# Cross-attention with sparsemax and a cosine/sine layer: the three products of the 32-token tile on four column tiles, with new order constants

## The chip, the core and the metric

The kernel runs on one core of a Trainium2 chip. The core has five engines that run side by side and meet through semaphores: PE (TensorE, matrix products; its weight loads are a row of their own in the profile, PEld), DVE (VectorE), ACT (ScalarE), POOL (GpSimd) and SP (SyncE, which here only issues transfers). The metric is the device time of one execution in microseconds. Before the change, three runs gave 622.4, 619.33 and 619.13, median 619.33.

## What is computed

Eight batches of 100 query tokens with 512 features attend to 722 context tokens each, in 16 heads of 32 features. The weights come from sparsemax (a threshold tau is subtracted from each row of scores, and what is negative becomes zero) in place of softmax. Then a layer with the cosine of one matrix and the sine of another follows. Cut to what matters:

```python
def sparsemax(x):                      # x: (8, 16, 100, 722)
    ...                                # tau so that the clipped row sums to 1
    return jnp.clip(x - tau, 0.0)

qh, kh, vh = heads(layernorm(x) @ Wq + bq), heads(ctx @ Wk + bk), heads(ctx @ Wv + bv)
attn = sparsemax(einsum('bhqd,bhkd->bhqk', qh, kh) * 32 ** -0.5)
x = x + merge(einsum('bhqk,bhkd->bhqd', attn, vh)) @ Wo + bo
real = layernorm(x) @ cos(theta + theta_noise)
imag = layernorm(x) @ sin(phi + phi_noise)
out = x + sqrt(real * real + imag * imag)
```

All of it is in 32-bit floats.

## The kernel before

**Tiles of tokens.** The 800 query tokens (8 x 100) are cut into seven tiles, `TILES = (128, 128, 128, 32, 128, 128, 128)` (line 29), across the batches' borders. What is done per token (norm, queries, output product, residual, second norm, cosine and sine products, root, result) is done per tile. The fourth tile, tokens 384 to 415, has only 32 tokens; its last steps can start when batch 4 (tokens 400 to 499) has its attention outputs.

**A batch.** What is done per batch: keys (`keys`, four products into eight pieces) and values (`values`, six pieces of the context); five `fill`s of scores into the four-bank PSUM tile `psc`, each copied to SBUF by ACT (`fill copy`, tile `s_t`) and searched by DVE (`tops`, the eight largest of each of 24 segments, 16 MAX8 instructions at a time). From the candidates DVE makes a first bound, and five rounds improve it: `above` (DVE compares candidates with the bound), `above values` (POOL multiplies), `above count` (DVE counts), `update` or `update far` (DVE sums POOL's product and moves the bound). `parts` (POOL), `parts T` (PE) and `parts copy` (ACT) bring the bounds into place for `weights` (PE: scores again, minus the bound, five groups into `psc`), `weights relu` (ACT) and `outputs` (PE). The last batch makes its bounds in three portions, so that its weights can begin earlier.

**The tile's last steps.** `last_steps` (line 934) adds for each tile: `output product` (line 936, `product` with `wo_sb`), `load x again` and `add bo`, `residual` (DVE adds the product in PSUM to x), the second norm with its transposition and copy, two `ffn` products with `cos_sb` and `sin_sb`, a `square` of each on ACT, their sum on POOL, the square root on ACT, and `result`, in which POOL adds x and sends the rows out. `product` (line 499) has the tile's transposed activations as weights of the array (128 x tokens) and streams 512 columns of the matrix, in four chunks of 128 features that add up in PSUM. A matmul in 32-bit floats is two records in the profile, so one product is 8 records. With the 32-token tile only 32 of the array's 128 columns hold weights.

[...]

**What sets the order.** Nothing is issued where it is written. `add` makes a `Task` with its engine and an assumed cost from `STEPS` (line 93); `hold` states which buffer slots it takes and which tasks free them. `Plan.order` (line 275) then plays the program through with these assumed costs. On each engine the task that can start first is taken; among those that can start at the same moment, the one with the smallest `due`:

```python
t.due = t.batch * PERIOD - t.rank + LAG.get(t.kind, 0.0)
stay = STAY if engine == "PE" and t.shape == shape else 0.0
key = (max(start, now + WINDOW), t.due - stay)
```

`rank` is the assumed length of what depends on the task, `LAG` (line 157) a constant per kind of task, `STAY` (line 154) a bonus for a PE task of the shape that the array has just had, `PERIOD` (line 155) the distance between batches. The tasks are issued in the order of their planned starts; each engine then works through its queue in that order and waits where something isn't ready.

Of the kernel before, what the change touches and what calls it, by code (L numbers as in the profile page):

```python
# [11 lines left out]
FP = mybir.dt.float32  # L12
# [3 lines left out]
AF = mybir.ActivationFunctionType  # L16
ALU = mybir.AluOpType
# [3 lines left out]
B, Q, S, DM = 8, 100, 722, 512  # L21
HD = 32
P = 128
NG = DM // P
HG = P // HD
# [10 lines left out]
FS = 16  # L36
# [7 lines left out]
def fills_of(left_first):  # L44
# [91 lines left out]
    "outputs bias": ("ACT", 0.05, 0.28),  # L136
    "output product": ("PE", 3.43),
    "residual": ("DVE", 0.65),
    "stats 2": ("DVE", 0.85),
    "ffn": ("PE", 3.43),  # L140
    "square": ("ACT", 0.57),
# [7 lines left out]
}  # L149


SHAPE = {"fill": 1, "fill last": 2, "outputs": 2, "weights": 3}
CHANGE = (0.19, 0.1, 0.1, 0.1)
STAY = 175.0
PERIOD = 121.0
WINDOW = 0.0
LAG = {
    "above": 260.0,
    "above count": -180.0,
    "above values": -150.0,  # L160
    "add bo": -5.0,
    "bounded": -75.0,
    "candidates": -190.0,
    "checks": 30.0,
    "deviation": 165.0,
    "ffn": 300.0,
    "fill": -240.0,
    "fill copy": 30.0,
    "fill last": -235.0,
    "first bound": 270.0,  # L170
    "keys": -65.0,
    "keys bias": 280.0,
    "keys part": -285.0,
    "leftovers": 250.0,
    "load bias": 205.0,
    "load ctx": 295.0,
    "load part": 120.0,
    "load w": 200.0,
    "load x": -160.0,
    "load x again": 180.0,  # L180
    "losses": 250.0,
    "normed": -80.0,
    "normed 2": -110.0,
    "normed T": -65.0,
    "normed copy": -245.0,
    "output product": 235.0,
    "outputs": -205.0,
    "outputs bias": 70.0,
    "parts": -180.0,
    "parts T": -165.0,  # L190
    "parts copy": -240.0,
    "parts copy last": -285.0,
    "queries": -285.0,
    "queries bias": -215.0,
    "residual": -55.0,
    "rests": 130.0,
    "result": 150.0,
    "sines": -300.0,
    "square": -215.0,
    "square sum": 275.0,  # L200
    "stats": 100.0,
    "stats 2": 265.0,
    "tops": 240.0,
    "turned": 160.0,
    "turns": -255.0,
    "update": 55.0,
    "update far": 155.0,
    "values": 110.0,
    "values copy": -200.0,
    "weights": -80.0,  # L210
    "weights relu": 300.0,
}


# [13 lines left out]
class Plan:  # L228
# [9 lines left out]
    def add(self, kind, emit, *after, tiles=1):  # L238
        t = Task(kind, emit, after, tiles)
        t.batch = self.batch  # L240
        self.tasks.append(t)
        for a in after:
            self.edge(a, t)
        return t
# [78 lines left out]
def xattn_ffn(  # L323
# [18 lines left out]
    nc = tc.nc  # L342
# [47 lines left out]
    def load_ctx_part(st, b, c):  # L390
# [4 lines left out]
    wq_sb, wk_sb, wv_sb, wo_sb, cos_sb, sin_sb = (  # L395
        const.tile([P, NG, DM], FP, name=n)
        for n in ("wq_sb", "wk_sb", "wv_sb", "wo_sb", "cos_sb", "sin_sb")
    )
# [88 lines left out]
    def queries_bias(tk, pieces):  # L487

        for st, at, q, n in pieces:
            if "q" not in st:  # L490
                st["q"] = work.tile([P, NG, Q], FP, name="q_t", bufs=3)
            nc.vector.tensor_tensor(
                st["q"][:, :, q : q + n],
                tk["pq"][:, :, at : at + n],
                bq_sb[:, :, None].to_broadcast([P, NG, n]),
                ALU.add,
            )

    def product(tk, name, lhs, w_sb):
        tk[name] = ps1.tile([P, DM], FP, name="pm")[: tk["n"]]  # L500
        for c in range(NG):
            nc.tensor.matmul(  # L502
                tk[name],
                lhsT=tk[lhs][:, c, :],
                rhs=w_sb[:, c, :],
                start=(c == 0),
                stop=(c == NG - 1),
            )

    def residual(tk):  # L510
        nc.vector.tensor_tensor(tk["x"], tk["py"], tk["x"], ALU.add)

    def square(tk, k):
        tk["sq", k] = rows.tile([P, DM], FP, name="sq", tag="sq", bufs=2)[: tk["n"]]
        nc.scalar.activation(tk["sq", k], tk["pr", k], AF.Square)  # L515

    def square_sum(tk):
        nc.gpsimd.tensor_tensor(tk["sq", 0], tk["sq", 0], tk["sq", 1], ALU.add)  # L518

    def root(tk):  # L520
        nc.scalar.activation(tk["sq", 0], tk["sq", 0], AF.Sqrt)
# [354 lines left out]
    add, hold = plan.add, plan.hold  # L876
# [56 lines left out]

    def last_steps(tk, outs):

        py = add("output product", lambda: product(tk, "py", "oT", wo_sb), *outs, *w["o"])
        xi = add("load x again", lambda: set_x(tk), tk["normed"])
        bo_in = add("add bo", lambda: add_bo(tk), xi, w["bo"])
        rs = add("residual", lambda: residual(tk), py, bo_in)
        hold("pm", py, [rs])  # L940
        _, hT2_in, hT2 = norm_steps(tk, rs, " 2")
        prs, sqs = [], []
        for k, w_sb in enumerate((cos_sb, sin_sb)):
            pr = add(
                "ffn",
                lambda k=k, w_sb=w_sb: product(tk, ("pr", k), "hT", w_sb),
                hT2, sines_done[k],
            )
            s = add("square", lambda k=k: square(tk, k), pr)
            hold("pm", pr, [s])  # L950
            prs.append(pr)
            sqs.append(s)
        hold("hT", hT2_in, prs)
        ss = add("square sum", lambda: square_sum(tk), *sqs)
        rt = add("root", lambda: root(tk), ss)
        at, n = tk["at"], tk["n"]
        rz = add("result", lambda: result(tk, out.rearrange("b q d -> (b q) d")[at : at + n]), rt)
        hold("n_t", sqs[0], [rz])
        hold("n_t", sqs[1], [ss])
        hold("x", xi, [rz])  # L960
        return py

    w = {}
    sines_done, turned_before = [], []
    for b in range(B):
# [30 lines left out]
        for g in range(NG):  # L996
            for i in range(2):
                early = b == 0 and 2 * g + i < EARLY
                if early:
                    k = first_keys[-1]  # L1000
                else:
                    k = add("keys", lambda st=st, g=g, i=i: keys(st, g, i), *c_in, *w["k"])
# [10 lines left out]
        for n, (pieces, _) in enumerate(st["fills"]):  # L1013
            cs = [c for c, *_ in pieces]
            if LEFT in cs:
                f = add("fill last", lambda st=st, n=n: fill(st, n), ql_in, *q_in, *ks.values())
                hold(f"ql{par}", ql_in, [f])
            else:
                gs = {divmod(HG * c + k, QB)[0] for c in cs for k in range(HG)}
                f = add(  # L1020
                    "fill", lambda st=st, n=n: fill(st, n), *q_in, *[ks[g, i] for g in gs for i in range(2)],
                    tiles=FS,
                )
            segments = FS if len(cs) == 1 or LEFT not in cs else NC3 * SEG % FS + LS
            e = add("fill copy", lambda st=st, n=n: fill_copy(st, n), f, tiles=segments)
            fills.append(f)
            hold("psc", f, [e])
            ts = [
                add("tops", lambda st=st, n=n, j=j: tops(st, n, j), e, tiles=segments)
                for j in range(HG)  # L1030
            ]
            hold("s", e, ts)
            for c in cs:
                done_tops[c] += ts
            top_steps += ts
# [4 lines left out]
        for lo, hi in ((0, HG + 1), (HG + 1, 2 * HG + 1), (2 * HG + 1, NT)) if b == B - 1 else ((0, NT),):  # L1040
# [8 lines left out]
            for reach in REACH:  # L1049
                m = add("above", lambda st=st, r=r: above(st, **r), t, tiles=hi - lo)  # L1050
                p = add("above values", lambda st=st, r=r: above_values(st, **r), m, tiles=hi - lo)
                n = add("above count", lambda st=st, r=r: above_count(st, **r), m, tiles=hi - lo)
# [3 lines left out]
                    p, n, tiles=hi - lo,  # L1056
# [39 lines left out]
        outs, ws, all_o, first_o = [], [], [], {}  # L1096
        for n, pairs in enumerate(PAIRS):
# [4 lines left out]
                tiles=len(pairs),  # L1102
# [57 lines left out]
        for tk, at, q, n in st["out"]:  # L1160
# [6 lines left out]
            if tk["at"] + tk["n"] <= (b + 1) * Q:  # L1167
                py = last_steps(tk, tk["outs"])
# [33 lines left out]
    again = small.tile([1, 1], I32, name="again", bufs=1)  # L1202
    nc.vector.tensor_scalar(again, most, 0.5, None, ALU.is_gt)
    flag = nc.values_load(again[0:1, 0:1], min_val=0, max_val=1)
    with tc.If(flag > 0):
        with tc.For_i(0, B) as b:
            st = {"c": load_ctx(b)}
            tk = {"x": load_x(x[ds(b, 1)].rearrange("o q d -> q (o d)"), Q), "n": Q}
# [25 lines left out]
            for c in range(NC3 + 1):  # L1234
# [4 lines left out]
                for j in range(HG if c < NC3 else 1):  # L1239
                    n = 1 + HG * c + j if c < NC3 else 0  # L1240
# [88 lines left out]
```

## Time and profile before

The execution that was profiled took 617.21 us, of which the span from first to last instruction is 615.6.

| | before |
|---|---|
| median of three runs | 619.33 us (619.13 to 622.4) |
| profiled execution | 617.21 us, span 615.6 us |
| mean granted clock of PE | 0.994 of full speed |
| instructions in the span | 17162 |
| HBM traffic | 23.76 MB read, 1.64 MB written |
| chain that ended last | PE 46%, DVE 39%, issue 7%, POOL 5% |

A row of the profile names the engine, the line of the kernel, the operation, the tile written and the tile read, their shapes, and how many such instructions were merged. [...] "Issue" in the chain is time in which the profile shows nothing that was waited for.

### The profile page before, as it was taken

What the parts mean: (1) busy time and instruction counts of PE and PEld (TensorE: products, weight loads), DVE (VectorE), ACT (ScalarE), POOL (GpSimd) and SP (SyncE); (2) the same over time, 40 slices, a digit from 0 to 9 for tenths busy, and PEclk for the clock granted to TensorE, in tenths of its full rate; (3) what the DMA queues carried; (4) which work ended last, traced back from release to release, by engine and by line L of the source; (5) the groups of instructions that cost most, each with busy time, mean ns of one, the idle gap of its engine ahead of it and who ended that gap; (6) DMA issues with size and microseconds to landing.
All of it is one profiled execution on the core that took longest, in us unless ns stands there. A gap on an engine that the chain in (4) does not pass through costs nothing.

```text
span 615.6 us, 17162 instructions
## 1 busy us (share of the span) xinstructions
PE 590.9 (96%) x6497; PEld 330.5 (54%) x6497; DVE 520.5 (85%) x3198; ACT 257.5 (42%) x355; POOL 226.3 (37%) x296
## 2 busy tenths in 40 slices
PE   5999999899999999999999999999999999999974
PEld 3755445556555655566466644675457434555531
DVE  2079999999999999997899989998999899998210
ACT  1244542355354435441644343552545334443521
POOL 1688487765500450024311650025211440165021
PEclk9999999999999999999999999999999999999998
DMA  8920012002000110002010102000030000000000
GB/s 307 364 92 19 18 56 78 18 19 98 19 2 3 40 60 2 3 2 97 19 37 2 41 2 98 3 2 1 3 132 3 0 23 2 2 20 2 2 18 21
DMA packets 12264, 26.56 MB, mean 43 GB/s; under 512 B 1856, under 2 KB 1856, under 8 KB 12176
## 3 DMA queue, kind: packets, MB, share of 16 engines
q1 hardware_dynamic: 11664, 23.77, 11.3%
q0 software_dynamic: 512, 1.64, 0.7%
q8 instruction: 53, 0.87, 0.6%
q14 instruction: 35, 0.29, 0.2%
HBM read 23.76 MB, written 1.64 MB: 41 GB/s over the span
## 4 chain that ended last, share of the span: by engine, by line
PE 46%; DVE 39%; issue 7%; POOL 5%; ACT 1%; DMA 1%; SPq 0%; POOLq 0%; DVEq 0%; ACTq 0%
DVE cand L639 19%; PE pm L581 12%; PE pm L559 12%; PE pm L502 5%; DVE f L727 4%; DVE m L706 4%; PE psc L826 3%; PE pm L849 3%; PE psc L617 3%; DVE n L717 3%; PE pm L479 3%; POOL p L711 3%; PE psc L548 2%; DVE rest L648 1%; DVE t L674 1%
## 5 line engine op out<-in xcount | busy, mean ns | idle before, releaser
L639 DVE MAX8 cand<-s_t 128x8 f32<-128x30 f32 x2496 | 230.3, 174 | 3.5 <-ACT s_t L628 3.5
L711 POOL TENSOR_TENSOR p<-z,m 128x1040 f32<-128x1040 f32 (+2 forms) x50 | 89.1, 1785 | 271.4 <-DVE m L706 269.7
L581 PE MATMUL pm<-wv_sb,c_t 128*121 128x512 f32 (+1 forms) x384 | 174.7, 600 | 0.0
L559 PE MATMUL pm<-c_t,wk_sb 128*128 128x361 f32 x464 | 150.9, 473 | 0.0
L559 PEld LDWEIGHTS pm<-c_t,wk_sb 128*128 128x128 f32 x464 | 84.5, 189 | 52.3 <-issue 7.6
L581 PEld LDWEIGHTS pm<-wv_sb,c_t 128*121 128x121 f32 (+1 forms) x384 | 67.2, 183 | 82.8 <-issue 78.3
L838 ACT ACTIVATE aT<-psc 121x2000 f32<-121x2000 f32 (+1 forms) x40 | 70.8, 1771 | 53.6 <-PE psc L826 53.6
L628 ACT COPY s_t<-psc 128x1924 f32<-128x1924 f32 (+2 forms) x40 | 69.0, 1725 | 47.9 <-DVE cand L639 23.7
L594 ACT COPY v_t<-pm 121x512 f32<-121x512 f32 (+1 forms) x48 | 28.1, 586 | 93.8 <-PE pm L581 93.8
L570 ACT ACTIVATE k_t<-pm,bk_sb 128x361 f32<-128x361 f32 x60 | 33.6, 565 | 71.1 <-PE pm L559 70.9
L727 DVE TENSOR_REDUCE f<-p 128x13 f32<-128x1040 f32 (+2 forms) x50 | 50.7, 1013 | 9.5 <-POOL p L711 9.5
L717 DVE TENSOR_REDUCE n<-m 128x13 f32<-128x1040 bf16 (+2 forms) x50 | 50.7, 1013 | 1.1
L826 PE MATMUL psc<-q_t,k_t 32*121 32x100 f32 (+1 forms) x1536 | 46.8, 262 | 0.0
L849 PEld LDWEIGHTS pm<-aT,v_t 121*32 121x32 f32 (+1 forms) x1536 | 32.7, 109 | 24.7 <-issue 21.7
L826 PEld LDWEIGHTS psc<-q_t,k_t 32*121 32x121 f32 (+1 forms) x1536 | 45.9, 180 | 0.2
L617 PE MATMUL psc<-k_t,q_t 32*32 32x481 f32 (+1 forms) x1536 | 43.2, 474 | 0.0
L849 PE MATMUL pm<-aT,v_t 121*32 121x100 f32 (+1 forms) x1536 | 41.7, 251 | 1.2 <-ACT aT L838 1.2
L479 PEld LDWEIGHTS pm<-hT,wq_sb 128*128 128x128 f32 x224 | 28.2, 191 | 8.2 <-issue 6.3
L479 PE MATMUL pm<-hT,wq_sb 128*128 128x128 f32 (+1 forms) x224 | 29.5, 277 | 0.0
L502 PE MATMUL pm<-cos_sb,hT 128*128 128x512 f32 (+1 forms) x56 | 27.5, 636 | 0.7 <-ACT hT L469 0.7
L518 POOL TENSOR_TENSOR sq<-sq 128x512 f32<-128x512 f32 (+1 forms) x7 | 8.8, 1264 | 48.7 <-ACT sq L515 48.6
L617 PEld LDWEIGHTS psc<-k_t,q_t 32*32 32x32 f32 x1536 | 13.9, 103 | 23.1 <-issue 15.4
(298 smaller groups left out, 570.9 us busy)
## 6 DMA issues: line engine op xcount, KB each, us to landing
c_t<-in_ctx SPq DMA_DIRECT2D x7, 1444.0 KB, 6.3
x_t<-in_x SPq DMA_DIRECT2D x12, 256.0 KB, 2.9
out<-sq POOLq DMA_DIRECT2D x6, 256.0 KB, 2.9
c_t<-in_ctx SPq DMA_DIRECT2D x4, 361.0 KB, 6.2
wk_sb<-in_L_xattn_Wk SPq DMA_DIRECT2D x4, 256.0 KB, 5.5
wq_sb<-in_L_xattn_Wq SPq DMA_DIRECT2D x4, 256.0 KB, 6.3
cos_sb<-in_L_ffn_theta SPq DMA_DIRECT2D x4, 256.0 KB, 3.9
n_t<-in_L_ffn_theta_noise SPq DMA_DIRECT2D x4, 256.0 KB, 3.6
```

Of the source, the lines that this page charges most:

```text
L479: nc.tensor.matmul(tk["pq"][:, g, : tk["n"]], lhsT=wq_sb[:, c, g * P : (g + 1) * P], rhs=tk["hT"][:, c, :], start=(c == 0), stop=(c == NG ...
L559: nc.tensor.matmul(pk, lhsT=wk_sb[:, c, g * P : (g + 1) * P], rhs=st["c"][:, c, i * SH : (i + 1) * SH], start=(c == 0), stop=(c == NG - 1),)
L581: nc.tensor.matmul(pv[:n], lhsT=st["c"][:, k, c * CK : c * CK + n], rhs=wv_sb[:, k, :], start=(k == 0), stop=(k == NG - 1),)
L617: nc.tensor.matmul(psc[b * HD : (b + 1) * HD, j, at : at + EDGE[hi] - EDGE[lo]], lhsT=st["q"][r, g, qb * HD : (qb + 1) * HD], rhs=st["k"][ ...
L628: nc.scalar.copy(s_t[:, :, :n], st["psc"][:, :, :n])
L639: nc.vector.max(st["cand"][:, n, k, :], st["s", f][:, j, at + EDGE[k] - first : at + EDGE[k + 1] - first],)
L711: nc.gpsimd.tensor_tensor(st["p"][:, lo:hi], st["z"][:, lo:hi], st["m"][:, lo:hi], ALU.mult)
L717: nc.vector.tensor_reduce(n_t, st["m"][:, lo:hi], AX.X, ALU.add)
L727: nc.vector.tensor_reduce(s_t, st["p"][:, lo:hi], AX.X, ALU.add)
L826: nc.tensor.matmul(psc[:m, j, k * Q : (k + 1) * Q], lhsT=st["k"][r, g, lo : lo + m], rhs=st["q"][r, g, :], start=False, stop=(k == len(PAI ...
L838: nc.scalar.activation(st["aT", n][:CK, :, :w], st["psw"][:CK, :, :w], AF.Relu, scale=SCALE)
L849: nc.tensor.matmul(st["po", g][j * HD : (j + 1) * HD, :Q], lhsT=st["v"][:m, c, f : f + HD], rhs=aT[:m, j, k * Q : (k + 1) * Q], start=(c = ...
```

## The change

For the tile with 32 tokens (`tk["n"] == HD`) the three products become `small_product`: for each of the four chunks of features, four matmuls take the same 32 columns of weights, each with another 128 of the 512 columns of the matrix, and write to partitions 0, 32, 64 and 96 of the product's PSUM tile. A product is thus 16 matmuls of 128 columns in place of 4 of 512, and its result is 128 x 128 in place of 32 x 512. The residual picks the four pieces out of PSUM one after the other and adds each to its 128 columns of x. Squares and their sum work on the 128 x 128 layout; the root reads the four pieces in turn and puts them back into rows of 512, in the second of the two `sq` buffers, which is therefore held until the result has been sent, while the first is free after the root. Kinds and assumed costs are added for these steps. The assumed cost of a fill that takes scores of two groups is raised by the factor 1.4. `STAY` goes from 175 to 235, `PERIOD` from 121 to 108, and every `LAG` gets a new value, so the order of the whole program is another.

```diff
+    "small product": ("PE", 0.95),
+    "small residual": ("DVE", 0.9),
+    "small square": ("ACT", 0.3),
+    "small sum": ("POOL", 0.45),
+    "small root": ("ACT", 1.1),
...
-SHAPE = {"fill": 1, "fill last": 2, "outputs": 2, "weights": 3}
+SHAPE = {"fill": 1, "fill last": 2, "outputs": 2, "small product": 2, "weights": 3}
-STAY = 175.0
-PERIOD = 121.0
+STAY = 235.0
+PERIOD = 108.0
 LAG = {
-    "above": 260.0,
-    "above count": -180.0,
-    "above values": -150.0,
+    "above": -65.0,
+    "above count": -55.0,
+    "above values": -5.0,
...
-    "ffn": 300.0,
-    "fill": -240.0,
+    "ffn": 245.0,
+    "fill": -300.0,
...
-    "fill last": -235.0,
-    "first bound": 270.0,
-    "keys": -65.0,
+    "fill last": -295.0,
+    "first bound": -180.0,
+    "keys": -60.0,
...
+    "small product": -220.0,
+    "small residual": -245.0,
+    "small root": 300.0,
+    "small square": 175.0,
+    "small sum": -270.0,
...
-    "tops": 240.0,
+    "tops": 300.0,
...
-    "update": 55.0,
-    "update far": 155.0,
-    "values": 110.0,
+    "update": 150.0,
+    "update far": 300.0,
+    "values": 200.0,
...
-    "weights": -80.0,
-    "weights relu": 300.0,
+    "weights": -130.0,
+    "weights relu": -260.0,
...
+    def small_product(tk, name, lhs, w_sb):
+        tk[name] = ps1.tile([P, DM], FP, name="pm")[:, :P]
+        for c in range(NG):
+            for j in range(HG):
+                nc.tensor.matmul(
+                    tk[name][j * HD : (j + 1) * HD],
+                    lhsT=tk[lhs][:, c, :],
+                    rhs=w_sb[:, c, j * P : (j + 1) * P],
+                    start=(c == 0),
+                    stop=(c == NG - 1),
+                )
+
+    def small_residual(tk):
+        for j in range(HG):
+            x_j = tk["x"][:, j * P : (j + 1) * P]
+            nc.vector.tensor_tensor(x_j, tk["py"][j * HD : (j + 1) * HD], x_j, ALU.add)
+
+    def small_square(tk, k):
+        tk["sq", k] = rows.tile([P, DM], FP, name="sq", tag="sq", bufs=2)
+        nc.scalar.activation(tk["sq", k][:, :P], tk["pr", k], AF.Square)
+
+    def small_sum(tk):
+        a, b = tk["sq", 0][:, :P], tk["sq", 1][:, :P]
+        nc.gpsimd.tensor_tensor(a, a, b, ALU.add)
+
+    def small_root(tk):
+
+        for j in range(HG):
+            nc.scalar.activation(
+                tk["sq", 1][:HD, j * P : (j + 1) * P], tk["sq", 0][j * HD : (j + 1) * HD, :P], AF.Sqrt
+            )
+        tk["sq", 0] = tk["sq", 1][:HD]
...
     def last_steps(tk, outs):
-        py = add("output product", lambda: product(tk, "py", "oT", wo_sb), *outs, *w["o"])
+        small = tk["n"] == HD
+        if small:
+            py = add("small product", lambda: small_product(tk, "py", "oT", wo_sb), *outs, *w["o"])
+        else:
+            py = add("output product", lambda: product(tk, "py", "oT", wo_sb), *outs, *w["o"])
...
-        hold("n_t", sqs[0], [rz])
-        hold("n_t", sqs[1], [ss])
+        hold("n_t", sqs[0], [rt] if small else [rz])
+        hold("n_t", sqs[1], [rz] if small else [ss])
...
-                    tiles=FS,
+                    tiles=FS * (1.0 if len(cs) == 1 else 1.4),
```

More of the change, by code (lines that the diff above doesn't have):

```diff
@@ L149 @@
 }
-SHAPE = {"fill": 1, "fill last": 2, "outputs": 2, "weights": 3}
+SHAPE = {"fill": 1, "fill last": 2, "outputs": 2, "small product": 2, "weights": 3}
 CHANGE = (0.19, 0.1, 0.1, 0.1)
-STAY = 175.0
-PERIOD = 121.0
+STAY = 235.0
+PERIOD = 108.0
 WINDOW = 0.0
 LAG = {
-    "above": 260.0,
-    "above count": -180.0,
-    "above values": -150.0,
[L161 to L165, printed above, removed]
-    "ffn": 300.0,
-    "fill": -240.0,
-    "fill copy": 30.0,
-    "fill last": -235.0,
-    "first bound": 270.0,
-    "keys": -65.0,
[L172 to L186, printed above, removed]
+    "above": -65.0,
+    "above count": -55.0,
+    "above values": -5.0,
+    "add bo": -205.0,
+    "bounded": -145.0,
+    "candidates": 40.0,
+    "checks": 150.0,
+    "deviation": -55.0,
+    "ffn": 245.0,
+    "fill": -300.0,
+    "fill copy": -25.0,
+    "fill last": -295.0,
+    "first bound": -180.0,
+    "keys": -60.0,
+    "keys bias": 230.0,
+    "keys part": -130.0,
+    "leftovers": 225.0,
+    "load bias": -100.0,
+    "load ctx": 270.0,
+    "load part": -105.0,
+    "load w": -105.0,
+    "load x": -215.0,
+    "load x again": 55.0,
+    "losses": 270.0,
+    "normed": 95.0,
+    "normed 2": 45.0,
+    "normed T": 65.0,
+    "normed copy": 70.0,
+    "output product": 155.0,
@@ L187 @@
     "outputs": -205.0,
[L188 to L191, printed above, removed]
+    "outputs bias": 200.0,
+    "parts": -215.0,
+    "parts T": -250.0,
+    "parts copy": 290.0,
     "parts copy last": -285.0,
[L193 to L202, printed above, removed]
-    "tops": 240.0,
@@ L204 @@
-    "turned": 160.0,
-    "turns": -255.0,
-    "update": 55.0,
-    "update far": 155.0,
-    "values": 110.0,
-    "values copy": -200.0,
-    "weights": -80.0,
-    "weights relu": 300.0,
+    "queries": -175.0,
+    "queries bias": 115.0,
+    "residual": 270.0,
+    "rests": -40.0,
+    "result": 145.0,
+    "root": -20.0,
+    "sines": -285.0,
+    "small product": -220.0,
[3 more added lines that the diff above has]
+    "small sum": -270.0,
+    "square": -225.0,
@@ L212 @@
+    "square sum": 210.0,
+    "stats": 245.0,
+    "stats 2": -300.0,
+    "tops": 300.0,
+    "turned": 245.0,
+    "turns": 165.0,
+    "update": 150.0,
+    "update far": 300.0,
+    "values": 200.0,
+    "values copy": -40.0,
+    "weights": -130.0,
+    "weights relu": -260.0,
 }
@@ L934, in last_steps @@
     def last_steps(tk, outs):
-        py = add("output product", lambda: product(tk, "py", "oT", wo_sb), *outs, *w["o"])
+        small = tk["n"] == HD
[3 more added lines that the diff above has]
+            py = add("output product", lambda: product(tk, "py", "oT", wo_sb), *outs, *w["o"])
         xi = add("load x again", lambda: set_x(tk), tk["normed"])
         bo_in = add("add bo", lambda: add_bo(tk), xi, w["bo"])
-        rs = add("residual", lambda: residual(tk), py, bo_in)
+        if small:
+            rs = add("small residual", lambda: small_residual(tk), py, bo_in)
+        else:
+            rs = add("residual", lambda: residual(tk), py, bo_in)
         hold("pm", py, [rs])
@@ L944, in last_steps @@
             pr = add(
-                "ffn",
-                lambda k=k, w_sb=w_sb: product(tk, ("pr", k), "hT", w_sb),
+                "small product" if small else "ffn",
+                lambda k=k, w_sb=w_sb: (small_product if small else product)(tk, ("pr", k), "hT", w_sb),
                 hT2, sines_done[k],
             )
-            s = add("square", lambda k=k: square(tk, k), pr)
+            if small:
+                s = add("small square", lambda k=k: small_square(tk, k), pr)
+            else:
+                s = add("square", lambda k=k: square(tk, k), pr)
             hold("pm", pr, [s])
@@ L953, in last_steps @@
         hold("hT", hT2_in, prs)
-        ss = add("square sum", lambda: square_sum(tk), *sqs)
-        rt = add("root", lambda: root(tk), ss)
+        if small:
+            ss = add("small sum", lambda: small_sum(tk), *sqs)
+            rt = add("small root", lambda: small_root(tk), ss)
+        else:
+            ss = add("square sum", lambda: square_sum(tk), *sqs)
+            rt = add("root", lambda: root(tk), ss)
         at, n = tk["at"], tk["n"]
         rz = add("result", lambda: result(tk, out.rearrange("b q d -> (b q) d")[at : at + n]), rt)
-        hold("n_t", sqs[0], [rz])
-        hold("n_t", sqs[1], [ss])
+        hold("n_t", sqs[0], [rt] if small else [rz])
+        hold("n_t", sqs[1], [rz] if small else [ss])
         hold("x", xi, [rz])
```

## The prediction

> **What bounds the kernel now.** I read the page's busy line first, then the busy time by stage (edges at landmarks of the chain of waits), then who waits for whom.
>
> ```profile
> PE 590.9 (96%) x6497; PEld 330.5 (54%) x6497; DVE 520.5 (85%) x3198; ACT 257.5 (42%) x355; POOL 226.3 (37%) x296
> ```
>
> ```profile
> 42.00:366.00 324.00, 320.94 (x3558) 181.47 (x3556) 308.36 (x1868) 142.52 (x190) 139.77 (x162) 1.00 0.09 31
> 366.00:410.00 44.00, 42.74 (x592) 24.79 (x592) 43.37 (x353) 21.75 (x29) 3.42 (x7) 1.00 0.11 36
> 410.00:508.00 98.00, 98.00 (x1040) 52.01 (x1032) 91.88 (x533) 41.79 (x59) 34.44 (x43) 1.00 0.08 26
> 508.00:569.00 61.00, 61.00 (x732) 31.94 (x735) 57.58 (x333) 25.73 (x40) 19.98 (x35) 1.00 0.02 6
> 569.00:590.40 21.40, 20.00 (x342) 12.19 (x334) 3.23 (x11) 10.35 (x13) 1.50 (x9) 1.00 0.01 2
> 590.40:615.60 25.20, 13.24 (x33) 5.54 (x29) 2.70 (x7) 3.68 (x7) 6.19 (x6) 0.86 0.07 24
> ```
>
> Columns: stage, length, then busy us of PE, weight loads, DVE, ACT, POOL, and PE's granted clock. From 42 to 569 us **two engines are full together**: PE has 522.7 of 527 us, DVE 501.2. Of DVE's other 25.8 us, the gaps over 0.4 us in its timeline make 14.3; the rest are steps of some hundredths between instructions. After 569 DVE's search for the bounds is over and PE works off what it still owes.
>
> ```profile
> DVE f L727 <- POOL p L711: 9.5, 15, 1.3
> DVE cand L639 <- ACT s_t L628: 3.5, 4, 1.5
> DVE h_t L455 <- PE pm L463: 3.5, 2, 2.4
> ```
>
> These are DVE's waits that matter inside the full stretch. Summing its timeline's gaps there: some 8.4 us wait for POOL (gaps over 0.4 us before `update`'s reduction, 0.8 each as a rule) and about 5.4 us are PE's lateness (1.05 before a normalisation, 1.83 before a residual, 1.54 and 1.01 before tops). So a faster PE has little DVE idling to remove: its gain must come there and from the tail.
>
> **The products: removed and put in their place.** The tile of 32 tokens has its products at 452.21 (output), 487.48 and 492.90 (ffn).
>
> ```profile
> 487.48 3.62 PE L502 MATMUL pm<-cos_sb,hT 128*32 128x512 f32 x8
> 491.03 0.69 PE L617 MATMUL psc<-k_t,q_t 32*32 32x241 f32 x32
> 491.65 1.46 PE L606 MATMUL psc<-k_t,ql 128*32 128x181 f32 x32
> 492.90 3.60 PE L502 MATMUL pm<-sin_sb,hT 128*32 128x512 f32 x8
> ```
>
> The columns are start, length, engine, line and shape; a start-to-start distance is the price, since lengths overlap. Cosine costs 491.03 − 487.48 = 3.55, sine (to 496.43) 3.53, output 452.21 to 455.67 = 3.46: **10.54 us of PE**. A product is 8 records (4 chunks, 2 each). The new one has 16 matmuls, 32 records of 128 columns into four 32-partition strips. The L606 row above is the same form, 32 records of K=128 and 32 weight columns into four strips, only with 181 columns: 492.90 − 491.65 = 1.25, in other places 1.39 (103.19 to 104.58). Times 128/181 that is 0.88 to 0.98. The outputs give a second row:
>
> ```profile
> 460.66 0.85 PEld L849 LDWEIGHTS pm<-aT,v_t 117*32 117x32 f32 x40 [0.51 <-ACT sd L449]
> 460.66 1.07 PE L849 MATMUL pm<-aT,v_t 117*32 117x100 f32 x40
> ```
>
> Forty records of 100 columns take 1.00 (next line's start, 461.66); times 32/40 and 128/100: 1.02. I take 1.0. Entering strips from full columns costs something: eight value records before strips take 3.63 (541.23 to 544.86), sixteen before others 6.97 (551.44 to 558.41), 3.48 per eight: 0.15. [...] New sum: 3 × 1.0 to 3 × 1.15 = 3.0 to 3.45; **PE saves 7.1 to 7.5 us**, I take 7.2.
>
> [...]
>
> **The vector and scalar pieces.** No row reads one strip and writes another, so these are estimates from unshifted rows. Residual: one instruction of 0.676 (L511) becomes four of 128 columns; between 0.183 at 13 columns (L804) and 0.676 at 512 the line gives 0.30. In a row the next DVE instruction starts 0.09 early (505.00 + 0.67 against 505.58): 4 × 0.21 = 0.84. [...] Squares: two of 0.597 become some 0.36 (L863 has 0.345 at 100 columns), ACT −0.5. Sum: POOL 1.265 to about 0.46 (0.23 at 16 columns, L764), −0.8. Root: 0.63 becomes four of 0.27 to 0.36, +0.5 to +0.8 on ACT, which is 42% busy; behind it on ACT stand copies with slack of a microsecond or more, unless a fill copy that DVE waits for is next: then up to 0.8 once. The second "sq" buffer is held until the result has been added and sent, about 2.5 us longer; the tile next to take it comes tens of us later. DMAs stay as they are.
>
> **Where 7.2 us can come out.** With the old order fixed, from 430 on DVE has no wait for PE at all, only three for POOL (at 483, 488, 493; 0.8 each), because the next batch's fills come only at 486.46 and no tops are there to lie under POOL's product. PE gets 2.4 us ahead from the output product, so fills come near 484 and two waits are covered: −1.6. Both ffn products are past by 497, and PE then owes 7.2 us less at 569. There, the wo product of tile 5 (569.58 to 573.12) keeps the last transpose of `parts` waiting from 570.9 (POOL done 570.62, plus latency) to 573.12: −2.2 when it is gone. Of the last three groups of weights and outputs (574.3 to 590.4), two carry an ffn product each in the gap of `weights relu`; only what outlasts the relu (1.84 and 1.50, plus latency) is late: 1.5 + 1.9 = 3.4. To bring these forward, tile 5's residual, statistics and normalisation (0.69 + 0.69 + 0.18 + 0.16 + 0.55 = 2.3 us of DVE) must come before 569 and push DVE's end: 1.1 net. I count 0.6, half of it. Less 0.4 for the residual: 1.6 + 2.2 + 0.6 − 0.4 = **−4.0**. The other 3.2 us land where PE was early anyway. Last comes the 25 us chain of the last tile, unchanged.
>
> **The order constants** move everything, by an amount no row can give. What they say can be read: among steps that can start at once the smaller due goes first. "Above" falls from 260 to −65, "first bound" from 270 to −180, while "tops" rise from 240 to 300 and fills fall to −300: each batch's rounds go before further tops, and PE fills as early as it can. STAY 235 for 175 makes PE change shape less: each avoided pair is worth 0.1 to 0.2. I count −0.3; its bounds are −4 and +9, the latter from the rival below.
>
> Forecast: −4.3 on the profiled execution's 617.21 (span 615.6 and 1.6 around it) = 612.9, span 611.3. The median of the runs shown is 2.1 above that execution: 619.33 − 4.3 = **615.0**. Chance 0.43, own range 611.5 to 617.5.
>
> **Rivals.**
> - *All of it lands*: PE is the bound everywhere, both ffn products leave the tail, the order covers more POOL waits: −7.2 and some shape changes, 611. For it: PE's 98.00 of 98 us. Against: DVE's fullness. 0.15.
> - *DVE hides it*: DVE's end stays near 569, the tail is chained anyway: 619. For it: no DVE wait for PE after 430. Strips running serially, at 4 us a product, would end here too (620.7), but the rows all but exclude that. 0.15.
> - *Slower: rounds lose their cover.* There are 35 full-width rounds; POOL's product (2.16) outlasts the count (1.24 + 0.24), so an uncovered round costs 0.8. About ten are uncovered now. If due dates that put rounds ahead of tops, or fills that come too late for the next batch, uncover 11 more, DVE's end moves +8.8: 619.33 − 4.3 + 8.8 = 624. It decides from six more rounds on (4.8 > 4.3). For it: the whole order is new and DVE has no slack. Against: the earliest start goes first, so waiting tops fill any gap. 0.27.
>
> **Numbers.** A measurement tells about 0.5%, 3.1 us, from no change: faster is below 616.2, slower above 622.4. Faster: 0.41 of the forecast's 0.43 and 0.15 make 0.56; same: 0.02 + 0.13 = 0.15; slower: 0.27 + 0.02 = 0.29. Range 608.5 to 624.5: below lies 0.06, above 0.13.
>
> **What would show it.** Right: 96 records of 128 columns in three stretches of 0.95 to 1.15; PE busy near 584; DVE's waits for POOL below 9.5 us; DVE's last update near 567; from there to the end below 46. Wrong on price: a product above 1.5. Wrong on order: more than 15 waits for POOL, or tops waiting for scores. Wrong on transmission: PE's idle grows by 7 us and the span stays.

## The result: no change that can be told

| | before | after |
|---|---|---|
| median (20 runs each) | 619.34 us (617.23 to 622.4) | 620.21 us (616.67 to 625.38) |
| ratio, 95% interval | | 1.0019 (0.9994 to 1.0043) |
| profiled execution, span | 617.21, 615.6 us | 620.99, 619.2 us |
| mean granted clock of it | 0.994 | 0.985 |
| DVE's last update ends, and from there to the end | 568.98, 46.6 us | 570.67, 48.5 us |

The page's rows of busy time and of PE's clock in the changed kernel, and the clock's row before:

```profile
PE 588.2 (95%) x6569; PEld 333.3 (54%) x6569; DVE 520.5 (84%) x3201; ACT 257.0 (42%) x358; POOL 225.9 (36%) x296
...
PEclk9999999999999999999999999999999999999788
```

```profile
PEclk9999999999999999999999999999999999999998
```

PE is busy 2.7 us less than before, not 7.2, and three slices of its clock are below full speed, before only the last. (In both, part of the last slice is a drop behind PE's last matmul: its clock is at half from 614.9, the last matmul is at 610.6; before from 612.0 and at 607.0. No matmul lies in it.) The busy time by stage of the changed kernel (columns as in the prediction, edges at its own landmarks):

```profile
410.00:510.00 100.00, 98.04 (x1153) 54.92 (x1152) 91.45 (x511) 41.24 (x66) 32.68 (x43) 1.00 0.08 25
510.00:570.70 60.70, 58.90 (x687) 30.12 (x687) 58.68 (x364) 25.54 (x38) 20.35 (x35) 1.00 0.02 6
570.70:594.20 23.50, 20.94 (x335) 14.24 (x331) 0.95 (x6) 10.38 (x14) 3.20 (x10) 0.79 0.01 2
594.20:619.20 25.00, 13.14 (x29) 5.33 (x29) 2.70 (x7) 3.03 (x6) 4.49 (x5) 0.85 0.06 23
```

From 410 to 571 PE now idles 3.8 us, where it had none to spare before, and behind the last update, to 594.2, it is granted 0.79 of its clock, where it had 1.00.

**The products cost what was forecast.** The changed kernel's timeline of PE (start, length, engine, line, shape, count):

```profile
413.08 1.08 PE L516 MATMUL pm<-wo_sb,oT 128*32 128x128 f32 x32
414.09 1.16 PE L490 MATMUL pm<-hT,wq_sb 128*128 128x128 f32 x8
...
436.03 1.08 PE L516 MATMUL pm<-cos_sb,hT 128*32 128x128 f32 x32
436.92 1.06 PE L516 MATMUL pm<-sin_sb,hT 128*32 128x128 f32 x32
438.08 0.70 PE L663 MATMUL psc<-k_t,q_t 32*32 32x241 f32 x32
```

Start to start they take 1.01, 0.89 and 1.16: 3.06 for 10.54, with the same 4096 columns in 32 records of 128 into four strips as in eight of 512 into one. The 7.5 us of work are gone; the rest of this document is about where the time went instead.

**Half the clock.** The changed kernel's windows of 2 us around and behind its last update (window, length, PE's busy time, granted clock, DMA share, GB/s):

```profile
566.00:568.00 2.00, 1.14 (x37) 1.00 0.00 0
568.00:570.00 2.00, 1.06 (x44) 1.00 0.00 0
570.00:572.00 2.00, 2.00 (x49) 0.63 0.03 8
572.00:574.00 2.00, 1.28 (x9) 0.50 0.00 0
574.00:576.00 2.00, 1.85 (x44) 0.50 0.00 0
576.00:578.00 2.00, 2.00 (x44) 0.50 0.00 0
578.00:580.00 2.00, 2.00 (x18) 0.50 0.00 0
580.00:582.00 2.00, 2.00 (x5) 0.81 0.03 8
```

If the clock steps from 1 to 0.5 within a window, its mean gives the moment: 2 x (1 - 0.63) / 0.5 = 1.48 us of 570 to 572 lie at half, so the step is at 570.52; likewise the clock is back at 580.76. That is 10.2 us, behind two idle places of 0.47 and 1.33 us. A second such stretch goes from 594.40 to 597.84, 3.4 us, behind an idle place of 1.69. The matmuls behind these places (the bracket is the idle time ahead, and what ended it):

```profile
568.94 1.07 PE L895 MATMUL pm<-aT,v_t 121*32 121x100 f32 x40 [1.33 <-ACT aT L884]
...
593.22 0.90 PE L895 MATMUL pm<-aT,v_t 121*32 121x100 f32 x32 [1.69 <-ACT aT L884]
```

Before has one such stretch ahead of PE's last matmul, 598.32 to 601.72, 3.4 us, behind 2.93:

```profile
597.02 0.63 PE L463 MATMUL pm<-ident,h_t 128*128 128x128 f32 x4 [2.93 <-DVE h_t L455]
598.32 5.38 PE L502 MATMUL pm<-cos_sb,hT 128*128 128x512 f32 x8 [0.68 <-ACT hT L469]
```

The four steps of the changed kernel lie 10.24, 13.64 and 3.44 us apart, near 3, 4 and 1 times 3.41 (their sum, 27.32, over 8). A piece of this length at half is called a window below; before's stretch of 3.4 us is one. Ahead of the changed kernel's two stretches lie 0.47 and 1.33 us of idling, and 1.69, less than 2 us ahead of either. Nor does every lost window follow idling: inside the long stretch PE has one gap, 0.86 us at 573.3, and from 574.15 on none, and yet the clock stays at half up to 580.76.

The price of one window stands in the changed kernel's timeline of PE:

```profile
594.04 5.40 PE L548 MATMUL pm<-wo_sb,oT 128*128 128x512 f32 x8
...
603.61 3.70 PE L548 MATMUL pm<-cos_sb,hT 128*128 128x512 f32 x8 [0.68 <-ACT hT L480]
```

Both are products of eight records of the same shape; the first lies in the half-clock stretch and takes 1.70 us more. PE's time can now be balanced. In the stretches at half it is busy for 12.8 us (before: 3.4), and half of that is counted as added time, as in that product: 6.4 us for 1.7, so 4.7 more by this estimate. Some 7.5 us of work went, 4.7 came back as slower work, and PE's idle time grew by 6.3 (span less busy time: 31.0 for 24.7): -7.5 + 4.7 + 6.3 = 3.5, and the profiled span is 3.6 longer. That is the prediction's own sign of being wrong "on transmission", with the clock beside it.

Over the 20 runs the time goes with the mean clock: the three fastest, 616.7 to 616.9 us, have 0.991 to 0.995, the four at 0.979 took 623.1 to 625.4. A window at half lowers the mean over the execution by 0.5 x 3.4 / 619 = 0.0027, so between these two groups lie some five windows. By this estimate they cost 5 x 1.7 = 8.5 us; the means of the groups are 7.7 apart. That two things go together doesn't yet show which drives which; the sixth experiment does.

### The profile page after: what moved, and what is told of

Its sections match the earlier page's. It is cut to its first block, busy times and chain, and to the rows that moved or that the text cites. A ratio compares the mean times of both kernels' runs of the same rounds, so it can differ in the third digit from the quotient of the medians.

```text
span 619.2 us, 17305 instructions
## 1 busy us (share of the span) xinstructions
PE 588.2 (95%) x6569; PEld 333.3 (54%) x6569; DVE 520.5 (84%) x3201; ACT 257.0 (42%) x358; POOL 225.9 (36%) x296
## 5 line engine op out<-in xcount | busy, mean ns | idle before, releaser
L872 PE MATMUL psc<-q_t,k_t 32*121 32x100 f32 (+1 forms) x1536 | 48.3, 268 | 0.0
L872 PEld LDWEIGHTS psc<-q_t,k_t 32*121 32x121 f32 (+1 forms) x1536 | 47.4, 186 | 0.2
L557 DVE TENSOR_TENSOR x_t<-pm,x_t 128x512 f32<-128x512 f32 x6 | 4.1, 679 | 30.2 <-PE pm L548 30.2
L564 POOL TENSOR_TENSOR sq<-sq 128x512 f32<-128x512 f32 x6 | 7.6, 1266 | 58.1 <-ACT sq L561 58.1
```

Source lines behind the costliest of these rows:

```text
L872: nc.tensor.matmul(psc[:m, j, k * Q : (k + 1) * Q], lhsT=st["k"][r, g, lo : lo + m], rhs=st["q"][r, g, :], start=False, stop=(k == len(PAI ...
```

## The experiments

Two theories stood against each other. **Gaps**: the removed work had filled gaps of PE; each gap now costs a wait, or half the clock behind it. **Order**: the new constants make a bad order, and the small products only pay for it.

### The small products alone, and the order alone

First, before with the new product, residual, squares and root for the 32-token tile, called from the old functions, so that every task keeps its place:

```diff
     def product(tk, name, lhs, w_sb):
+        if tk["n"] == HD:
+            return small_product(tk, name, lhs, w_sb)
```

> The order of before, task for task; only the 32-token tile's products, residual, squares, sum and root are the new small ones, in the old places. Theory A (the saved PE time lay where DVE sets the pace, and the new order then lost time of its own): PE is some 7 us less busy in 452 to 497 us, DVE's last update comes only 1 to 3 us earlier than the 569.0 of before, time 616 to 618.5. Theory B (the small pieces themselves cost what the products save, on ACT and DVE): 619 to 622. Theory C (the saving is real and only the clock in the tail takes it back): 612 to 614 with a clock near 0.994.

Second, before with its wide products, under the new constants:

```diff
-STAY = 175.0
-PERIOD = 121.0
+STAY = 235.0
+PERIOD = 108.0
 ...
-                    tiles=FS,
+                    tiles=FS * (1.0 if len(cs) == 1 else 1.4),
```

> The old full-width products, with the new STAY, PERIOD, LAG and the factor 1.4 on fills. Theory A: the new order alone is worse than the old one, 622 to 628, so that the small products gain 3 us or more inside it. Theory B: the order is as good as the old one, 617 to 620, and the small pieces are what took the gain. Theory C: 622 to 627 with the clock as low as in the changed kernel (about 0.985).

Measured: small products alone 618.99 us (613.02 to 621.81), ratio 0.9986 (0.9968 to 1.0004); order alone 626.72 (621.27 to 630.21), ratio 1.0095 (1.0062 to 1.0128). Before has a median of 619.3 to 619.7 beside each group of runs in this document, so kernels of different groups are compared directly. With before at 619.4 and both at 620.2, the order costs 7.3 us with the old products and 1.2 with the small ones. The small products bring 0.4 in the old order and 6.5 in the new. The two parts don't add up: either theory alone is too simple. Of the expectation's theories for the small products alone none fits: 618.99 lies between A and B, while the profiled execution, 613.02 at a clock of 0.994, is the fastest of the 14 and lies in C.

DVE's timeline in the kernel with the order alone shows where the order hurts (the execution profiled, 630.21, is the slowest of its nine, but its clock is full up to 574, behind this place):

```profile
493.56 0.17 DVE L734 SCALAR_TENSOR_TENSOR t0 0_6784<-f,n 128x13 f32<-128x13 f32 x1
503.57 0.69 DVE L517 TENSOR_TENSOR x_t<-pm,x_t 128x512 f32<-128x512 f32 x1 [9.83 <-PE pm L508]
```

The new order sets the residual of tile 5 between the rounds and the last batch's first tops; before had it in the tail. Its output product is not done, and DVE stands for 9.83 us. In the changed kernel the same wait, at 494.64, is 3.13: all three small products lie ahead of it. Of the 7.3 us, about 3.8 are waits (the two executions at a clock of 0.995 took 621.3 and 621.6, against 617.6 for before with its clock held, below); the rest goes with the clock, as far as this shows, which was 0.981 to 0.991 in the other seven.

In the old order with small products, PE's timeline has the new gaps:

```profile
451.97 1.08 PE L503 MATMUL pm<-wo_sb,oT 128*32 128x128 f32 x32
454.01 1.07 PE L892 MATMUL pm<-aT,v_t 121*32 121x100 f32 x40 [0.96 <-ACT aT L881]
455.01 0.44 PE L856 MATMUL psc<-tT,neg_b 3*121 3x100 bf16 x8
455.28 1.20 PE L869 MATMUL psc<-q_t,k_t 32*117 32x100 f32 x40
458.22 1.18 PE L602 MATMUL pm<-c_t,wk_sb 128*128 128x361 f32 x3 [1.73 <-DMA c_t<-in_ctx]
```

PE saves 2.4 us at the output product and stands 0.96 for the relu, then 1.73 for the context of the last batch, whose load starts at 450.68 (before: 450.92). The first fill of the last batch comes at 486.64; before had it at 486.46.

### Is it the waits of the new order?

Third, the small tile's first square gets another buffer. In the changed kernel ACT's timeline reads:

```profile
438.40 0.30 ACT L531 ACTIVATE sq<-pm 128x128 f32<-128x128 f32 x1
441.20 0.28 ACT L531 ACTIVATE sq<-pm 128x128 f32<-128x128 f32 x1 [2.51 <-DMA out<-sq]
442.04 1.27 ACT L540 ACTIVATE sq<-sq 32x128 f32<-32x128 f32 x4 [0.56 <-POOL sq L535]
443.22 0.45 ACT L824 COPY tT<-pm 128x384 bf16<-128x384 bf16 x1
443.57 0.68 ACT L839 COPY tT<-pm 32x16 bf16<-32x16 bf16 x4
444.28 1.57 ACT L674 COPY s_t<-psc 128x1688 f32<-128x1688 f32 x1
```

The second square waits 2.51 us for the transfer of the tile ahead, which still reads its `sq` buffer. Behind it in ACT's queue stands the copy of a fill whose matmuls were in place, and PE waits 1.66 us for `psc` at 445.90.

```diff
     def small_square(tk, k):
-        tk["sq", k] = rows.tile([P, DM], FP, name="sq", tag="sq", bufs=2)
+        tk["sq", k] = (
+            rows.tile([P, DM], FP, name="sq", tag="sq", bufs=2) if k else rows.tile([P, DM], FP, name="h_t")
+        )
```

> The changed kernel in its own order, with one buffer moved: the first square of the 32-token tile goes to the free buffer of the normalised rows, so that no square of it waits for the result transfer of the tile before (2.5 us on ACT at 438.7 to 441.2, with a score copy queued behind it). Theory: the score copy starts 2 us earlier, PE's wait of 1.7 to 2.3 us at 444 shrinks below 0.5, no clock drop follows there, and the median falls 1 to 3 us below the changed kernel's 620.2: 617 to 619. Rival (that wait is hidden, the time is set by the late load of the last batch's context and by the tail alone): 619.5 to 620.5.

Measured: 617.58 us (615.1 to 624.18), ratio 0.9977 (0.9957 to 0.9996): 2.6 us below the changed kernel. ACT's timeline then has both squares in a row, and PE's gap is 0.81 (below 0.5 was expected):

```profile
439.00 0.30 ACT L533 ACTIVATE h_t<-pm 128x128 f32<-128x128 f32 x1
439.17 0.30 ACT L533 ACTIVATE sq<-pm 128x128 f32<-128x128 f32 x1
441.62 1.27 ACT L542 ACTIVATE sq<-h_t 32x128 f32<-32x128 f32 x4 [2.15 <-POOL h_t L537]
```

ACT now waits at the root, for POOL's sum. This execution had been 0.6 us later up to there (436.87 against 436.26 for the score copy ahead), and still the next score copy starts at 444.02 for 444.28: 0.9 us gained. The gap can cost more than itself: in the profiles of the fourth and the sixth kernel, which keep the held square, it was 2.30 and 1.91 us, and the clock fell to half for 3.4 us behind it, from about 447 to 451; in the changed kernel's own profile it stayed at 1.00 there. So the 2.6 us can be read as 0.9 of waiting and up to one window of 1.7; this split is an estimate.

Fourth, three tops of the last batch are issued ahead of tile 5's residual, so that DVE has work where it waits 3.13 us, and ACT's step for that tile goes behind the copies of that place. In the issue loop:

```diff
-        for t in plan.order():
+        for t in tops_first(plan.order()):
```

> The changed kernel with one move in its order: three tops tasks of the last batch's first fill go ahead of the residual, second statistics and second norm of tile 5 of 7 (tokens 416 to 543), which DVE reaches at 494.6 and waits 3.1 us for; its deviation on ACT goes behind the copies of that place. Theory A: DVE's idle of about 4.5 us at 494 to 501 shrinks to about 1.5, its last update comes near 567.5 in place of 570.5, and the time falls 1.5 to 3.5 us below the changed kernel, unless the clock drops differently. Rival (PE's backlog, not DVE's end, sets the tail): within 1 us of the changed kernel.

Measured: 622.55 us (617.84 to 626.67), ratio 1.0048 (1.0026 to 1.0069). A miss. DVE waits 3.72 us at the same place, for the score copy: the wait only moves to the scores, which are no earlier than the product. It waits 2.75 more at 511.2 for another copy, whose matmuls end near 508.0 but which stands in ACT's queue behind a `square` that waits for its own product and starts at 511.69.

Fifth, the order from 413 to 495 is rewritten so that the values of batch 5 come first, which frees the context tile for the last batch's load (the load starts at 459.11 in the changed kernel). The first small square gets a buffer of its own, so that it doesn't disturb the result, and a small helper tile of DVE (`past`) has one buffer in place of two:

```diff
-        for t in plan.order():
+        for t in early_keys(plan.order()):
```

> The changed kernel with its order edited by hand between 413 and 495 us: the last value products of batch 5 come first, so that its context buffer is free and the last batch's context is loaded some 9 us earlier; one key product moves ahead; one ffn product of tile 3, the small tile's ffn products and a value product of batch 6 come after the last batch's keys. (The small tile's first square has a buffer of its own.) Theory (the late load is what the new order loses): load near 449 in place of 459, first fill of the last batch near 486 in place of 493, DVE's 4.5 us of idling at 494 to 501 below 1.5, its last update at 565.5 to 567.5, time 614.5 to 618. Rival (PE's total, not the order of these steps, sets the end): 619 to 621.

Measured: 623.31 us (620.9 to 626.75), ratio 1.0059 (1.004 to 1.0077). The load moved to 448.89 and the first fill to 485.80, but the work displaced came due elsewhere: PE idles 2.40 us at 434.8 and DVE 3.90 at 509.7 for the third score copy. The matmuls of that fill end near 507.7; its copy waits on ACT to 511.82, once more behind the `square` of a product. So the edit brought a stall of its own. The late load is not shown to be the cause, and the last experiment speaks against it.

### Is it the clock?

Sixth, the changed kernel with matmuls that nobody reads, put into PE's idle places of the tail. They write a PSUM tile that the real product then starts afresh. They are extra work, called fillers below, one to six such matmuls in a place, of some 0.5 us each:

```diff
+WARM = {0: 3, 1: 2, 4: 4, "norm": 6}
...
+    def warm(ps, k):
+        for _ in range(k):
+            nc.tensor.matmul(
+                ps[:, : 2 * P], lhsT=wq_sb[:, 0, :P], rhs=wq_sb[:, 1, : 2 * P], start=True, stop=True
+            )
```

> The changed kernel with extra matmuls that nothing reads (128x256 each, about 0.43 us): 3, 2 and 4 of them where PE waits for the relu in front of the outputs groups 0, 1 and 4 of the last batch, 6 before the last transposition and 1 before the last cosine product. If the drops of the granted clock after these idle stretches cost the changed kernel its 4 us (slow tail at 570 to 582 and 594 to 598): 614.5 to 617, clock 0.995 or more in every run and a spread below 3 us. If the drops have another cause, or cost nothing on the path: 620 or more, spread as in the changed kernel (617 to 625).

Measured: 617.51 us (616.38 to 619.68), ratio 0.9966 (0.9953 to 0.998), clock 0.991 to 0.995 in all 15 runs. More work, 2.7 us less time, and the spread falls from 8.7 to 3.3 us. It falls a little short of what was expected (617 at most, a clock of 0.995, a spread below 3): this kernel keeps the held square, and the one stretch at half that its profile shows ahead of PE's last matmul is the one from 447.5 to 450.9.

Seventh and eighth, the same for the small products in the old order and for before, each with its own places. The places at `parts` of batches 0 and 4, where PE idles up to 2 us for POOL, are filled with transposes (in the profile of the small products in the old order the clock is at half behind the first of them, from 119.1 to 122.5). The numbers for before and for the small products in the old order, whose new gaps at the small tile's products and the last batch's keys are filled too:

```diff
-WARM = {2: 2, ("norm", 544): 1, ("norm", 672): 6, ("parts", 0): 30, ("parts", 4): 20}
+WARM = {2: 1, "small": 2, "keys": 4, ("norm", 544): 2, ("norm", 672): 6, ("parts", 0): 30, ("parts", 4): 20}
```

> The small products in the old order (as e1), with unread matmuls where PE would idle: 2 ahead of each small product, 4 ahead of the last batch's first keys, 2 and 6 ahead of the last two tiles' second transpositions, 1 each ahead of the last cosine product and of the last batch's outputs group 2, and 30 and 20 unread bf16 transpositions ahead of the bounds' transposition in batches 0 and 4. Theory (the saving is there, and idle PE followed by a lower clock takes it back in most runs): 611 to 614.5, spread below 3.5 us, clock 0.993 or more. Rival (the 613 seen once in e1 was luck of another kind, such as the context transfer): 617 to 620 with the same spread of 8 us.

> The kernel before, with unread matmuls in its own idle places: 2 ahead of the last batch's outputs group 2, 1 and 6 ahead of the last two tiles' second transpositions, 1 ahead of the last cosine product, 30 and 20 bf16 transpositions ahead of the bounds' transposition in batches 0 and 4. Theory: it has only one drop near the end (the cosine product took 5.38 in place of 3.6), so 616.5 to 618.5, some 1 to 2.5 us less than before. Rival (clock drops don't matter on the path): 619 to 620.

Measured: small products in the old order 615.32 us (613.55 to 616.65), ratio 0.9928 (0.9901 to 0.9954); before 617.62 (616.25 to 619.01), ratio 0.9965 (0.9952 to 0.9977). All 30 executions have a clock of 0.994 or more. The first is a little above the expected 611 to 614.5, but clear of the rival's 617 to 620. With the clock held on both sides the small products bring 2.3 us (0.9963, by resampling the two sets of runs 0.9952 to 0.9983), where they brought 0.4 without; the fillers are worth 1.8 us to before and 3.7 to the kernel with the small products.

### Both repairs together

Ninth, the changed kernel with the other buffer of the third experiment and the unread matmuls of the sixth:

```diff
+WARM = {0: 3, 1: 2, 4: 4, "norm": 6}
...
+            rows.tile([P, DM], FP, name="sq", tag="sq", bufs=2) if k else rows.tile([P, DM], FP, name="h_t")
```

> The changed kernel with two repairs that each gained about 2.5 us alone: the small tile's first square in a buffer that no result transfer holds (its fast executions 615.1), and unread matmuls ahead of the last four parts of PE's tail (2 to 7 us of them are in PE's idle places). If the loss has these two places, the held square at 444 and the clock's drops behind the tail's idle places, the two add: 614.5 to 616, all executions within 3.5 us, granted clock .993 or more, and no 2-us slice below 0.8 between 440 and 460 or between 560 and the end. Rival, the new order has a wait of its own beside these: 617 or more with the clock at .993 or more, and DVE still waits 2 us and more for PE's output product near 495.

Measured: 614.87 us (613.73 to 616.52), ratio 0.9927 (0.9907 to 0.9947), clock 0.994 to 0.996. The gains of 2.6 and 2.7 add to 5.3. Against before with its own fillers (617.62) this kernel gains 2.7. The stages of this kernel:

```profile
508.00:568.30 60.30, 59.83 (x694) 30.87 (x696) 58.31 (x360) 25.17 (x38) 20.34 (x35) 1.00 0.02 6
568.30:588.00 19.70, 19.33 (x349) 12.94 (x341) 0.97 (x7) 10.29 (x13) 3.11 (x10) 1.00 0.01 2
```

From the last update to 588.0 PE is busy for 19.33 of 19.70 us, some 3 of them with fillers, at full clock throughout. DVE still waits 2.26 us for PE's product at 493.2, as the rival had it, but the time is that of the theory: this wait is not what the change lost. The context load starts at 456.75 and the first fill of the last batch comes at 490.67, 4.2 us later than in the kernel before, and yet the last update ends at 568.31, 0.7 earlier than there: the late load alone doesn't hold the end. One caution in reading these times: executions start differently. The first score copy is at 29.68 here and at 31.07 in the changed kernel's profile, so 1.4 of the 2.4 us by which this last update is earlier than that kernel's were there from the start.

## Why the prediction was wrong

The forecast was 615.0, 4.3 us below before; measured is 620.2, 0.9 above. The kernels measured form a path from one to the other, and each of its steps can be set against the prediction's term:

| step | medians | us | forecast |
|---|---|---|---|
| before gets its fillers | 619.4 to 617.6 | -1.8 | no term |
| its three products become small | 617.6 to 615.3 | -2.3 | -4.0 |
| new order, first square in another buffer | 615.3 to 614.9 | -0.4 | -0.3 |
| that square back in the held buffer | 614.9 to 617.5 | +2.6 | 0 |
| the fillers go: the changed kernel | 617.5 to 620.2 | +2.7 | no term |

Such a path adds up whatever happens; what it tells is the size of each step. The fillers differ from kernel to kernel, and -0.4 can't be told from nothing (8 runs against 6). The first and the last step together are the clock, +0.9. So three terms failed: the held square by 2.6, the products' worth in the old order by 1.7, the clock by 0.9.

**Right: the prices of the pieces.** The products at 1.0 each (measured 1.02 in the mean), with the weight loads beside the matmuls: the cosine's 32 loads lie within 0.81 us, inside the 0.89 of the product, as before's 40 loads of the outputs at 460.66 lie within 0.85, inside 1.07. The low end of the prediction's sum, 3 x 1.0, counts nothing for entering strips, which no run shows apart: cosine and sine in a row took 2.05, the output product alone 1.01. The residual's +0.4 on DVE is a term that no run ahead of the prediction shows; in the changed kernel four pieces take 1.10 from 414.59 to 415.69, for 0.676, which is +0.42, and more than the 0.84 estimated for them in a row. The root: 1.27 for 0.63, +0.64 of the +0.5 to +0.8.

**Failed: "The other 3.2 us land where PE was early anyway".** Idling was costed at nothing. It isn't free here: the clock had no term in the sum, though before's own profile has a stretch at half clock behind 2.93 us of idling (the 0.86 in the last row of the prediction's stages holds it). One window costs 1.7 us; the changed kernel's profile has four in the tail, before's has one. Holding the clock brings the changed kernel 2.7 us, more than before's 1.8. "The 25 us chain of the last tile, unchanged" held: 25.2 us from the last output product to the end in both profiles, each with one window at half.

**Failed, the largest: "the tile next to take it comes tens of us later"** and "up to 0.8 once". The prediction weighed the tile behind the small one. The wait lies ahead of it: the order sets the small tile's two products within 2 us, and its second square meets the transfer of the tile before. The stall is 2.51 us on ACT and 1.66 on PE, and removing it is worth 2.6.

**Mis-sized: the order constants at -0.3**, bounds -4 to +9. With the old products they cost 7.3, about 3.8 of it in waits, and with the small ones 1.2. The sign is that of the rival "Slower", the mechanism another: DVE's waits for POOL did not grow (9.5 us in 12 waits with the order alone, 8.5 in 10 in the changed kernel, for 9.5 in 15), so no rounds lost cover. The residual of tile 5 was put where its product is late, and the small tile's squares where a buffer is held. With the square's buffer changed and the clock held, no cost of the order can be told (614.9 for 615.3). That this lies near -0.3 is luck: the prediction saw neither the waits of the new order nor the held square that comes with it.

**The old-order sum, -4.0.** "PE gets 2.4 us ahead from the output product, so fills come near 484": they come at 486.64, since PE waits 1.73 for a load that starts no earlier; the waits for POOL at 483, 488 and 493 remain, and -1.6 became nothing. "-2.2 when it is gone": it came. The last transpose of `parts` runs at 570.68 for 573.12, and from the last update to the end it is 42.7 for 46.6; 1.7 of these 3.9 are before's half-clock window, which this execution didn't have, and 2.2 remain. The whole is 2.3 with the clock held, for 4.0.

**Left open**: what in the constants makes PE late for tile 5 with the old products. In the changed kernel, moving tops or the load gained nothing, and both edits met a score copy held up on ACT. Why only -2.3 of the -4.0 came in the old order is read from one profile, not tested. And what makes the clock fall stays open: the runs show that it fell behind 1.80 and 1.69 us of idling, not where the bound lies, and that it stayed at half from 574.15 to 580.76 without a gap, so that idle time alone is not the measure.

## What to carry to other kernels

Before work is taken off a nearly full engine, ask what each microsecond of it was filling: read the gaps it will leave, what stands in line ahead of and behind them, and what the clock does after such gaps now. Where PE idles 1 to 3 us on the path (here 1.33, 1.69 and 2.93), some matmuls that nobody reads can be worth more than the work saved (here 2.7 us in the changed kernel, for 2.3 by the small products with the clock held). And a new operation's buffer is to be checked against the user ahead of it as much as the one behind, with the engine's queue in mind.

## What the hardware showed unexpectedly

The same idle time doesn't always cost the clock: 2.93 us ahead of the last normalised transposition did in before's profile (598.32 to 601.72 at half), and did not in that of the small products alone (idle from 591.7, then 1.00 up to 604). What decides between the two is not shown. The drops make most of the spread: 8.7 us over 20 runs of the changed kernel, 3.3 over the 15 with fillers, 2.8 over the six of its repaired version.
